# Graph attention over a dense adjacency: one fill order for the search, and the adjacency turned from a bfloat16 copy

## The chip, the cores and the metric

The kernel runs on one core of one Trainium2 chip. The metric is the device time of one execution in microseconds (us). Engines are named as in the profile: PE is TensorE's matmul and PEld its weight load, DVE is VectorE, ACT is ScalarE, POOL is GpSimd, SP is SyncE, which issues DMAs.

## The reference

Two layers over 3327 nodes with 128 features and a 0/1 adjacency. Each layer is added to its input and normalised.

```python
# layer 0
norm2 = jnp.linalg.norm(x, axis=1, keepdims=True)
cos = beta[0] * (x @ x.T) / (norm2 @ norm2.T + 1e-07)
P = softmax(cos + (1.0 - adj) * -1e9, axis=1)
x = layernorm(x + P @ x)
# layer 1: 128 attention heads of width 8
q = (x @ Wq.T).reshape(d, n, h)          # d = 128 heads, h = 8
k = (x @ Wk.T).reshape(d, n, h)
v = (x @ Wv.T).reshape(d, n, h)
a = jnp.einsum('dnh,dmh->dnm', q, k) * d ** -0.5
a = softmax(a + adj + adj, axis=2)
out = jnp.einsum('dnm,dmh->dnh', a, v).reshape(n, h * d)
x = layernorm(x + out @ Wo.T)
```

So layer 1 adds twice the adjacency to the scores, and its softmax needs the maximum of q.k over all nodes, or a bound for it.

## The kernel before

Nodes are padded to 26 tiles of 128. Node p * 26 + t is row p of tile t.

**Layer 0** runs over tiles with a software pipeline written out by hand (the loop at L418; the orders of PE, ACT, DVE and POOL are as written, SP's is not). In iteration t, tile t gets its scores, tile t - 1 its weights and their product, tile t - 2 its norm, tile t - 3 its projections to q, k, v. Tile t + 2 has its adjacency turned: `adj_chunk` (L207) transposes 26 blocks of the float32 tile `raw` on PE, four to a bank (`turn`, L159), ACT copies each bank into the bfloat16 tile `aT` (L213), and a DMA stores it to `aT_s` (L215). `raw` comes by a DMA from SP's queue (`load_adj`, L113), after POOL has set its padding column.

**Preparation** (`prepare`, L794) makes split copies of k and q by head: a DMA loads 16 heads into `nat`, POOL reorders them into `by_t`, PE transposes, ACT and DVE write a high and a low part, and DMAs store them to `kp_s` and `qp_s`. There are 16 such pieces. The first maxima of attention are put between them, and so are the loads of the first two units and of the first block's adjacency.

**Attention** runs over 288 units: a unit is one of nine blocks of query nodes (384 wide, the last 256) with four heads. A unit has 26 steps, one for each tile of key nodes (the loop at L872). The step does this, in this order on PE:

- `shifts` and `scores` of heads 2 and 3 into the two banks of `eb`; ACT exponentiates both at once into `pb` (L893), and POOL multiplies `pb` by the exponentiated adjacency `eT` (L894).
- `shifts` and `scores` of heads 0 and 1 into `ea`, then `add_adj`, which adds twice the adjacency on PE (L677); ACT exponentiates each of the two banks into `pa` (L923).
- `weigh` of the step two back: the products with the values, summed in the bank `acc` (L707).

Between these, PE also computes products q.k for the maxima of a later unit, 33 steps ahead, and DVE reduces them: `max_pair` (two heads into two banks, L613, L624) and `max_single` (one head into one bank, L634, L638). `max_steps` (L568) lists one pair and one single for each step in rounds of 52 steps, two units. Heads sit on row groups of the array, head a on rows 32a to 32a + 31. Where the pair's heads are 0 and 1, the pair stands between the shifts and scores of `eb` and the single between those of `ea`; otherwise the other way round:

```python
early = pair is not None and pair[1] == (0, 1)
```

At j = 20 of a unit `values_turn` turns the output of the unit before into a free corner of `ea`, and `finish` has ACT copy it, DVE take reciprocals (L741), POOL multiply (L742) and SP store it. `shift_parts` (L645) makes the shifts from the maxima at places 26 and 51 of the round, and at j = 22 to 24 `shift_turn` turns them.

**The end** (L949) loads the output rows, transposes them, multiplies by Wo, and adds x1 for each of the 26 tiles; then `layernorm` (L129) runs over all of them, and the result is stored. Here no engine's order is written by hand.

Of the kernel before, what the change touches and what calls it, by code (L numbers as in the profile page):

```python
# [46 lines left out]
def gnn_two_layers(  # L47
# [20 lines left out]
    nc.vector.tensor_scalar_mul(two, ident, 2.0)  # L68

# [11 lines left out]
    aT_s = dram.tile([T, P, T, P], BF16, name="aT_s")  # L81
# [31 lines left out]
    def load_adj(pool, t: int):  # L113

        raw = pool.tile([P, NP], F32, name="raw")
        nc.gpsimd.memset(raw[:, N:NP], PAD)  # L116
        if t < T - 1:
            nc.sync.dma_start(raw[:, :N], node_rows(adj, t, N))
        else:
            for a, b in FULL:  # L120
                nc.sync.dma_start(raw[a:b, :N], node_rows(adj, t, N, b - a, a))
            nc.sync.dma_start(raw[P - 1 : P, :N], node_rows(adj, t - 1, N, 1, P - 1))
        return raw
# [5 lines left out]
    def layernorm(dst: bass.AP, src: bass.AP):  # L129

        stats = small.tile([P, T, nc.vector.BN_STATS_DIM], F32, name="ln_stats", bufs=1)
        mv = small.tile([P, T, nc.vector.BN_AGGR_DIM], F32, name="ln_mv", bufs=1)
        rstd = small.tile([P, T], F32, name="ln_rstd", bufs=1)
        for t in range(T):
            nc.vector.bn_stats(stats[:, t, :], src[:, t, :])
            nc.vector.bn_aggr(mv[:, t, :], stats[:, t, :])
        nc.vector.tensor_scalar(rstd, mv[:, :, 1], EPS, None, op0=ALU.add)
        nc.scalar.activation(rstd, rstd, AF.Sqrt)
        nc.vector.reciprocal(rstd, rstd)
        for t in range(T):  # L140
            nc.vector.tensor_scalar(
                dst[:, t, :],
                src[:, t, :],
                mv[:, t, 0:1],
                rstd[:, t : t + 1],
                op0=ALU.subtract,
                op1=ALU.mult,
            )
# [24 lines left out]
    with ExitStack() as l0:  # L173
# [23 lines left out]
        def load(t: int):  # L197
            u = tiles[t]
            u.raw = load_adj(adj_raw, t)
            u.xr = ptp.tile([P, D], F32, name="xr", bufs=5)  # L200
            if t < T - 1:
                nc.sync.dma_start(u.xr, node_rows(x, t, D))
            else:
                nc.gpsimd.memset(u.xr, 0.0)
                nc.sync.dma_start(u.xr[: P - 1], node_rows(x, t, D, P - 1))

        def adj_chunk(t: int, c: int):  # L207

            u = tiles[t]
            if c == 0:  # L210
                u.aT = ptp.tile([P, T, P], BF16, name="aT", bufs=1)
            tp, a, b = turn(ps_tp, lambda k: every(u.raw, k), c)
            nc.scalar.copy(u.aT[:, a:b, :], tp)  # L213
            if c == NCH - 1:
                nc.sync.dma_start(aT_s[t], u.aT)  # L215
# [143 lines left out]
        with tc.manual_schedule(  # L359
# [25 lines left out]
            for t in range(3):  # L385
                load(t)
            ws = []
# [30 lines left out]
            for t in range(-2, T + 3):  # L418
# [4 lines left out]
                for k in range(8):  # L423
# [42 lines left out]
                    if k == 5 and there(t + 3) and t >= 0:  # L466
                        load(t + 3)

# [7 lines left out]
    with ExitStack() as at:  # L476
# [28 lines left out]
        def load_adj_tile(b, j):  # L505
            w = width(b)
            nc.sync.dma_start(
                aT[:, j, :w].rearrange("p (q n) -> p q n", n=P),
                aT_s[b * QT : b * QT + w // P, :, j].rearrange("q p n -> p q n"),
            )  # L510
# [57 lines left out]
        def max_steps(u, w):  # L568
# [18 lines left out]
            ones = one(u, hi, full[13:] + [left]) + one(u, lo, full[12:] + [left])  # L587
            pairs += [(u, hi, *k) for k in full[:13]] + [(u, hi, (2,), 6)]
            pairs += [(w, hi, *k) for k in full[:12]]
            ones += one(w, lo, full[13:] + [left])  # L590
            pairs += [(w, lo, *k) for k in full[:13]]
            ones += one(w, hi, full[12:] + [left])
            assert len(pairs) == len(ones) == 2 * T
            return list(zip(pairs, ones))
# [33 lines left out]
        def max_single(i, hs, qs, c):  # L628
# [6 lines left out]
            else:  # L635
# [7 lines left out]
                )  # L643

# [60 lines left out]
        def weigh(u, j, pts):  # L705
            for h in range(4):
                nc.tensor.matmul(  # L707
                    acc[32 * h : 32 * h + H + 1, : u.nq],
                    u.vt[:, h, j],
                    pts[h // 2][:, h % 2, : u.nq],  # L710
                    start=(j == 0),
                    stop=(j == T - 1),
                    tile_position=(0, 32 * h),
                )
# [20 lines left out]
        def finish(u, src):  # L735
            of = sm.tile([P, QT, 4, H + 1], F32, name="of")
            nc.scalar.copy(of[:, : u.nt].rearrange("p q h r -> p (q h r)"), src[:, : 36 * u.nt])
            by = of.rearrange("p q h r -> p h q r")[:, :, : u.nt]
# [23 lines left out]
        with tc.manual_schedule(  # L762
# [27 lines left out]
            with ExitStack() as pr:  # L790
# [3 lines left out]
                def prepare(g, src, dst):  # L794
                    nat = work.tile([P, HG, T * H], F32, name="nat")
                    nc.sync.dma_start(nat, heads(src)[g])
# [4 lines left out]
                    )  # L801

# [23 lines left out]
                for g in range(NG):  # L826
                    for src, dst in ((k_s, kp_s), (q_s, qp_s)):
                        prepare(g, src, dst)
                        for _ in range(3 if g > 1 else 0):
                            if k < T + AHEAD:  # L830
                                first_max(k)
                                k += 1
                    if g == 0:
                        us[0], us[1] = load_unit(0), load_unit(1)
                        for j in range(T):
                            load_adj_tile(0, j)
                    if 0 < g < 5:
                        for j in range(7 * (g - 1), min(7 * g, T)):
# [15 lines left out]
            unit = fix.tile([P, P], BF16, name="unit")  # L854
            nc.vector.tensor_copy(unit, ident)
# [16 lines left out]
            for s in range(NU * T + LAG):  # L872
                i, j = divmod(s, T)
                u = us.get(i)
                if u is not None:
# [6 lines left out]
                    early = pair is not None and pair[1] == (0, 1)  # L882
# [3 lines left out]
                    shifts(u, b01, (2, 3))  # L886
                    if early:
                        max_pair(*pair)
                    elif single is not None:
                        max_single(*single)  # L890
                    scores(u, j, b01, (2, 3), True)
# [9 lines left out]
                    shifts(u, e_a, (0, 1))  # L901
                    if early:
                        max_single(*single)
                    elif pair is not None:
                        max_pair(*pair)
                    scores(u, j, e_a, (0, 1), False)
# [9 lines left out]
                    if j == T - 6 and done is not None:  # L916
                        values_turn(done, free, False)
                        copies.append(lambda: finish(done, free))
# [7 lines left out]
                    todo.append((u, j, (pt_a, pt_b)))  # L926
# [19 lines left out]
            finish(done, e[:, 0])  # L946


    with ExitStack() as fi:  # L949
# [7 lines left out]
        hid = big.tile([P, T, D], F32, name="hid1")  # L957
        for t in range(T):
# [19 lines left out]
            nc.vector.tensor_add(hid[:, t, :], pp, x1)  # L978
        res = big.tile([P, T, D], F32, name="res")
        layernorm(res, hid)  # L980
        rf = res.rearrange("p t d -> p (t d)")
        for part, width in node_parts():
            nc.sync.dma_start(node_blocks(out, part, width), rf[part, :width])
# [38 lines left out]
```

## Time and profile before

| | us |
|---|---|
| Median of 3 runs (15734.61 to 15738.93) | 15735.61 |
| The profiled execution | 15731.62 |
| Its span, first to last instruction | 15729.8 |
| Stage: layer 0, start included | to about 712 |
| Stage: preparation | 712 to 986 |
| Stage: attention | 986 to about 15616 |
| Stage: the end | to 15729.8 |

The profile is of one execution. In a line of a group come the line of the kernel, engine, operation, what is written and read with its shape, and how often; then busy time in all and mean nanoseconds of one; then the idle time of the engine just before, and what ended it. In a timeline the first two numbers are start and length in us, and brackets hold the idle time before it. The ends of matmuls are modelled, so it is their starts that are read. "Place" below is the place in a round of 52 steps of the maxima that a step computes.

### The profile page before, as it was taken

Reading aid. Unit: us, or ns where it says so; the run is one execution under the profiler, and the core shown is the slowest. Engines: PE = TensorE matmul, PEld = TensorE weight load, DVE = VectorE, ACT = ScalarE, POOL = GpSimd, SP = SyncE. Lnnn points to the kernel's source line nnn. Section 1 sums busy time; section 2 is a strip of 40 time slices with the busy share of each in tenths; the row PEclk is TensorE's granted clock in tenths of the full one; section 3 lists DMA queues with packets and bytes.
Section 4 is the critical chain, followed back from the end, with each engine's and each line's share of the span. In section 5 each row is a group of like instructions: output and inputs, shape, how many; then the busy total and the mean of one; then the engine's idle time right before and its main releaser. Section 6 shows DMA issues by size and latency. Waiting matters only on the chain.

```text
span 15729.8 us, 508048 instructions
## 1 busy us (share of the span) xinstructions
PE 15442.3 (98%) x217532; PEld 6909.7 (44%) x217532; DVE 13882.2 (88%) x16261; ACT 12687.4 (81%) x24930; POOL 13894.1 (88%) x9571
## 2 busy tenths in 40 slices
PE   8879999999999999999999999999999999999999
PEld 6644444444444444444444444444444444444555
DVE  7679999999999999999999999999999999998775
ACT  7658888888888888888888888888888888888776
POOL 0059999999999999999999999999999999999886
PEclk9989999999999999999999999999999999999999
DMA  4451111111111111111111111111111111111112
GB/s 169 180 201 49 45 49 52 49 46 49 52 50 49 47 50 52 49 45 49 52 49 46 49 53 48 50 45 56 45 49 45 49 52 49 46 49 60 61 56 74
DMA packets 600521, 951.50 MB, mean 60 GB/s; under 512 B 283090, under 2 KB 515408, under 8 KB 557808
## 3 DMA queue, kind: packets, MB, share of 16 engines
q1 hardware_dynamic: 598256, 918.99, 18.0%
q8 instruction: 1703, 27.90, 0.7%
q14 instruction: 562, 4.60, 0.1%
HBM read 784.19 MB, written 134.61 MB: 58 GB/s over the span
## 4 chain that ended last, share of the span: by engine, by line
PE 91%; DVE 2%; ACT 1%; issue 0%; POOL 0%; DMA 0%; SPq 0%; ACTq 0%; DVEq 0%; POOLq 0%
PE acc L707 29%; PE ea L677 20%; PE m L598 15%; PE eb L690 12%; PE ea L690 9%; PE ea L696 2%; PE eb L696 2%; PE ea L663 1%; DVE mx L613 1%; PE ea L725 1%; DVE mx L634 1%; ACT pa L923 0%; PE pp L977 0%; POOL pb L894 0%; ACT pb L893 0%
## 5 line engine op out<-in xcount | busy, mean ns | idle before, releaser
L894 POOL TENSOR_TENSOR pb<-pb,eT 128x768 f32<-128x768 f32 (+1 forms) x7488 | 13206.6, 1781 | 752.7 <-ACT pb L893 557.7
L613 DVE TENSOR_REDUCE mx<-m 128x2 f32<-128x1024 f32 x6784 | 8271.6, 1219 | 506.9 <-PE eb L696 283.1
L893 ACT ACTIVATE pb<-eb 128x768 f32<-128x768 f32 (+1 forms) x7488 | 5895.6, 787 | 2509.9 <-PE eb L696 1716.6
L598 PE MATMUL m<-kx,qx 32*128 32x512 f32 (+1 forms) x23296 | 6774.5, 471 | 85.9 <-DVE mx L613 78.2
L923 ACT ACTIVATE pa<-ea 128x384 f32<-128x384 f32 (+1 forms) x14976 | 6339.0, 478 | 56.5 <-PE ea L677 43.5
L707 PE MATMUL acc<-pb,vt 128*9 128x384 f32 (+1 forms) x29952 | 5904.2, 474 | 0.1
L707 PE MATMUL acc<-pa,vt 128*9 128x384 f32 (+1 forms) x29952 | 5903.3, 474 | 0.0
L634 DVE TENSOR_REDUCE mx<-m 128x1 f32<-128x512 f32 x6400 | 4377.6, 684 | 682.2 <-PE m L598 316.3
L690 PEld LDWEIGHTS <-one 3*128 3x128 bf16 x29952 | 1508.1, 91 | 5553.9 <-issue 4650.8
L677 PE MATMUL ea<-aT,two 128*32 128x384 bf16 (+1 forms) x59904 | 3716.2, 325 | 0.0
L696 PE MATMUL eb<-qx,kx 32*128 32x384 f32 (+1 forms) x14976 | 3444.5, 452 | 0.0
L696 PE MATMUL ea<-qx,kx 32*128 32x384 f32 (+1 forms) x14976 | 3439.1, 437 | 0.0
L690 PE MATMUL ea<-cx,one 3*128 3x384 bf16 (+1 forms) x14976 | 3293.0, 322 | 2.3
L598 PEld LDWEIGHTS m<-kx,qx 32*128 32x128 f32 x23296 | 2813.9, 182 | 443.7 <-DVE mx L613 123.0
L690 PE MATMUL eb<-cx,one 3*128 3x384 bf16 (+1 forms) x14976 | 2462.7, 326 | 1.3 <-ACT pb L893 0.6
L707 PEld LDWEIGHTS acc<-pa,vt 128*9 128x9 f32 x29952 | 1416.7, 91 | 781.5 <-issue 0.3
L677 PEld LDWEIGHTS <-two 128*32 128x32 bf16 x59904 | 947.0, 95 | 1415.6 <-issue 1273.6
L696 PEld LDWEIGHTS eb<-qx,kx 32*128 32x128 f32 x14976 | 1461.7, 189 | 0.0
L696 PEld LDWEIGHTS ea<-qx,kx 32*128 32x128 f32 x14976 | 1433.1, 182 | 8.0 <-issue 3.0
L707 PEld LDWEIGHTS acc<-pb,vt 128*9 128x9 f32 x29952 | 1418.8, 91 | 0.6 <-POOL pb L894 0.6
L638 DVE TENSOR_REDUCE mx<-m 128x2 f32<-128x512 f32 x1088 | 747.9, 687 | 96.3 <-PE eb L696 38.2
L116 POOL MEMSET raw<- 128x1 f32 x26 | 2.4, 98 | 559.0 <-DVE mn L260 478.2
(126 smaller groups left out, 5253.8 us busy)
## 6 DMA issues: line engine op xcount, KB each, us to landing
kx<-kp_s SPq DMA_DIRECT2D x576, 832.0 KB
vn<-v_s SPq DMA_DIRECT2D x288, 416.0 KB
qx<-qp_s SPq DMA_DIRECT2D x1024, 48.0 KB
raw<-in_adj_dram SPq DMA_DIRECT2D x25, 1663.5 KB
aT_s<-aT SPq DMA_DIRECT2D x26, 832.0 KB
aT<-aT_s SPq DMA_DIRECT2D x208, 96.0 KB
q_s<-row SPq DMA_DIRECT2D x26, 512.0 KB
k_s<-row SPq DMA_DIRECT2D x26, 512.0 KB
```

Of the source, the lines that this page charges most:

```text
L598: nc.tensor.matmul(dst, u.qx[rows(a), q * P : (q + 1) * P], u.kx[rows(a), k0:k1], start=True, stop=True,)
L613: nc.vector.tensor_reduce(u.mx[:, h, qs[0], c], m, axis=AX.X, op=ALU.max)
L634: nc.vector.tensor_reduce(u.mx[:, a, qs[0], c : c + 1], m, axis=AX.X, op=ALU.max)
L638: nc.vector.tensor_reduce(u.mx[:, a, qs[0] : qs[1] + 1, c], m.rearrange("p (q k) -> p q k", q=2), axis=AX.X, op=ALU.max,)
L663: nc.tensor.matmul(dst[r], parts[u.i % 2][:, q, h], unit, start=start, stop=True, tile_position=(0, 32 * h), skip_group_check=True,)
L677: nc.tensor.matmul(e[r, : u.nq], two[:, r], aT[:, j, : u.nq], start=False, stop=True, tile_position=(0, 32 * c), skip_group_check=True,)
L690: nc.tensor.matmul(e[:, : u.nq], one[r], u.cx[r, : u.nq], start=True, stop=False, skip_group_check=True)
L696: nc.tensor.matmul(e[:, : u.nq], u.kx[rows(a), j * P : (j + 1) * P], u.qx[rows(a), : u.nq], start=False, stop=stop, skip_group_check=True,)
L707: nc.tensor.matmul(acc[32 * h : 32 * h + H + 1, : u.nq], u.vt[:, h, j], pts[h // 2][:, h % 2, : u.nq], start=(j == 0), stop=(j == T - 1), ...
L893: nc.scalar.activation(pt_b[:, :, : u.nq], e_b[:, :, : u.nq], AF.Exp)
L894: nc.gpsimd.tensor_tensor(pt_b[:, :, : u.nq], pt_b[:, :, : u.nq], eT[:, j, : u.nq].unsqueeze(1).to_broadcast([P, 2, u.nq]), ALU.mult,)
L923: nc.scalar.activation(pt_a[:, h, : u.nq], e[:, : u.nq], AF.Exp)
```

## The change

Seven edits go together.

1. `max_steps`: the list of singles is put in another order, so that no single's head is one of the pair's heads.
2. The step: in full blocks the pair always stands first, between the shifts and scores of `eb`, and `eb` takes the two heads that are not the pair's (`hs_b`), `ea` the pair's (`hs_a`). In the last, narrower block the single stands first.
3. `values_turn` moves from j = 20 to j = 8; `finish` is split in ACT's copy (`leave`, j = 8) and the rest (j = 9).
4. Layer 0: a second load of each adjacency tile, from POOL's queue, converts it to bfloat16 (`load_bits`, two buffers), and PE turns this copy by matmuls with the bfloat16 identity `unit` as the moving operand.
5. `aT_s` is laid out by blocks of three tiles: stores go in pieces of 256 bytes, and the loads of attention get one piece per row instead of three.
6. Preparation: `nat` is loaded two pieces ahead, and the adjacency loads of the first block are spread over four pieces.
7. The end: norm for each tile in the loop; the first 20 tiles are stored from within it.

```diff
+        def load_bits(t: int):
+            u = tiles[t]
+            u.bits = adj_raw.tile([P, NP], BF16, name="bits", bufs=2)
+            load_adj(u.bits, nc.gpsimd, t)
...
-            tp, a, b = turn(ps_tp, lambda k: every(u.raw, k), c)
-            nc.scalar.copy(u.aT[:, a:b, :], tp)
+            a, b = 4 * c, min(4 * c + 4, T)
+            tp = ps_tp.tile([P, 4, P], F32, name="tp")
+            for k in range(a, b):
+                nc.tensor.matmul(tp[:, k - a], every(u.bits, k), unit, start=True, stop=True)
+            nc.scalar.copy(u.aT[:, a:b, :], tp[:, : b - a])
             if c == NCH - 1:
-                nc.sync.dma_start(aT_s[t], u.aT)
+                q = t % QT
+                nc.sync.dma_start(aT_s[t // QT][:, :, q * P : (q + 1) * P], u.aT)
...
             for t in range(3):
                 load(t)
+            for t in range(2):
+                load_bits(t)
...
                     if k == 5 and there(t + 3) and t >= 0:
                         load(t + 3)
+                if there(t + 4) and t + 4 > 1:
+                    load_bits(t + 4)
...
-            nc.sync.dma_start(
-                aT[:, j, :w].rearrange("p (q n) -> p q n", n=P),
-                aT_s[b * QT : b * QT + w // P, :, j].rearrange("q p n -> p q n"),
-            )
+            nc.sync.dma_start(aT[:, j, :w], aT_s[b][:, j, :w])
...
-            ones = one(u, hi, full[13:] + [left]) + one(u, lo, full[12:] + [left])
+            last = one(w, hi, full[12:] + [left])
+            ones = one(u, hi, full[13:] + [left]) + last[:1] + one(u, lo, full[12:] + [left])
             pairs += [(u, hi, *k) for k in full[:13]] + [(u, hi, (2,), 6)]
             pairs += [(w, hi, *k) for k in full[:12]]
-            ones += one(w, lo, full[13:] + [left])
             pairs += [(w, lo, *k) for k in full[:13]]
-            ones += one(w, hi, full[12:] + [left])
+            ones += one(w, lo, full[13:] + [left]) + last[1:]
...
-                    early = pair is not None and pair[1] == (0, 1)
+                    full = pair is not None and width(units[pair[0]][0]) == QB
+                    first = pair if full else single
+                    late = single if full else pair
+                    hs_a = pair[1] if full else (0, 1)
+                    hs_b = tuple(h for h in range(4) if h not in hs_a)
...
-                    shifts(u, b01, (2, 3))
-                    if early:
-                        max_pair(*pair)
-                    elif single is not None:
-                        max_single(*single)
-                    scores(u, j, b01, (2, 3), True)
+                    shifts(u, b01, hs_b)
+                    search(first)
+                    scores(u, j, b01, hs_b, True)
...
-                    shifts(u, e_a, (0, 1))
-                    if early:
-                        max_single(*single)
-                    elif pair is not None:
-                        max_pair(*pair)
-                    scores(u, j, e_a, (0, 1), False)
+                    shifts(u, e_a, hs_a)
+                    search(late)
+                    scores(u, j, e_a, hs_a, False)
...
-                    if j == T - 6 and done is not None:
+                    if j == 8 and done is not None:
                         values_turn(done, free, False)
-                        copies.append(lambda: finish(done, free))
+                        copies.append(lambda: leave(done, free))
+                    if j == 9 and done is not None:
+                        copies.append(lambda: finish(done))
...
+                load_heads(0)
+                load_heads(1)
+                for i in range(len(works)):
+                    prepare(i)          # load_heads(i + 2) after POOL's copy
+                    if i == 1:
                         us[0], us[1] = load_unit(0), load_unit(1)
...
+                    if i % 2 and i < 9:
+                        for j in range(7 * (i // 2), min(7 * (i // 2) + 7, T)):
                             load_adj_tile(0, j)
...
-            nc.vector.tensor_add(hid[:, t, :], pp, x1)
-        res = big.tile([P, T, D], F32, name="res")
-        layernorm(res, hid)
+            hid = work.tile([P, D], F32, name="hid1")
+            nc.vector.tensor_add(hid, pp, x1)
+            layernorm(res[:, t, :], hid)
+            if t == HALF - 1:
+                nc.sync.dma_start(node_blocks(out, slice(0, P), HALF * D), rf[:, : HALF * D])
```

`layernorm` now takes one tile: bn_stats, bn_aggr, the addition of epsilon, ACT's root, reciprocal, and the final scaling.

## The prediction

> **What bounds the kernel now.** I read the page first, then busy time by stage, then the timeline of single attention steps, then groups with shapes kept apart.
>
> ```profile
> PE 15442.3 (98%) x217532; PEld 6909.7 (44%) x217532; DVE 13882.2 (88%) x16261; ACT 12687.4 (81%) x24930; POOL 13894.1 (88%) x9571
> ...
> PE 91%; DVE 2%; ACT 1%; issue 0%; POOL 0%; DMA 0%; SPq 0%; ACTq 0%; DVEq 0%; POOLq 0%
> ```
>
> TensorE carries the chain, but four engines stand above 80%, so the reader must ask stage by stage what holds it.
>
> ```profile
> 65.00:712.00 647.00, 611.95 (x3399) 478.46 (x3397) 541.27 (x830) 508.54 (x655) 2.40 (x24) 0.99 0.42 160
> 712.00:986.00 274.00, 121.33 (x540) 90.64 (x540) 135.93 (x215) 74.28 (x142) 51.37 (x30) 0.62 0.98 338
> ...
> 1083.00:14330.00 13247.00, 13225.12 (x189035) 5551.74 (x189031) 12085.33 (x13709) 10957.05 (x21294) 12610.58 (x8389) 1.00 0.16 49
> ...
> 15612.00:15704.00 92.00, 74.40 (x632) 66.29 (x620) 29.51 (x93) 16.05 (x31) 2.92 (x4) 0.94 0.58 173
> 15704.00:15729.80 25.80, 7.91 (x65) 7.24 (x64) 11.01 (x41) 3.26 (x5) 0.00 (x0) 0.76 0.21 69
> ```
>
> Columns: window, length, busy PE, PEld, DVE, ACT, POOL, clock, DMA share, GB/s. Layer 0 (to 712) is TensorE; the preparation of keys and queries (to 986) is the DMA engines, 0.98 busy; attention is 84% of the span; the end has a 26 us tail in which little runs.
>
> In attention a step is the distance between starts of eb<-cx,one on PE: 7488 steps. The full-width 6656 average 2.005 us, in rounds of 52 (two units). By place in the round they differ. In 26 places the pair search comes before the eb scores and the single before the ea scores ("pair first"), in the other 26 the reverse. Both settle at the same pace, in pairs of steps. For single first I read a loop over two steps: eb start to single reduction 0.538, to pair reduction 0.608, that one 1.215, to the next pair product 0.055, to the eb after it 1.517: 3.933, or 1.967 a step. For pair first: 0.554 + 1.137 + 0.683 + 0.057 + 1.511 = 3.942, or 1.971. So the banks that the search keeps until VectorE has reduced them set the pace, not TensorE's arithmetic alone. What stands out is where the order turns round:
>
> ```profile
> 5066.98 1.22 DVE L613 TENSOR_REDUCE mx<-m 128x2 f32<-128x1024 f32 x1
> ...
> 5067.75 0.34 PE L690 MATMUL eb<-cx,one 3*128 3x384 bf16 x2
> 5068.25 0.50 PE L598 MATMUL m<-kx,qx 32*128 32x512 f32 x2 [0.16 <-DVE mx L613]
> 5068.25 0.44 PE L696 MATMUL eb<-qx,kx 32*128 32x384 f32 x2
> ...
> 5068.79 1.23 DVE L613 TENSOR_REDUCE mx<-m 128x2 f32<-128x1024 f32 x1 [0.60 <-PE m L598]
> ...
> 5070.12 0.34 PE L690 MATMUL eb<-cx,one 3*128 3x384 bf16 x2
> ```
>
> A pair late in one step and first in the next: PE stands 0.50 us after its shifts until VectorE frees the two banks, VectorE then stands 0.60 us, and the step takes 2.37 us.
>
> **The change, part by part.**
>
> *Constant order, and singles of other heads.* Mean steps at places 12 to 15 are 2.161, 2.198, 2.060, 1.880, together 0.42 over four of 1.969; here the order turns and pair and single share a head (place 12: ea scores 0.33 us apart instead of together). Places 39 to 41, the other turn with the second clash just before it: 2.353, 2.067, 1.875, 0.39 over. The new code always puts the pair first, between the shifts and scores of the other two heads, and no single has a head of its pair. Both waits have no cause left: -0.81 a round. Against it, 26 steps move from 1.967 to 1.971: +0.10. There are 8 x 32 / 2 = 128 rounds: 128 x 0.71 = **-91 us**.
>
> *Output turn moved from j = 20 to 8, its finish split.* In pair-first steps places 0 to 6 (the maxima's parts, the output turn, three shift turns) cost 0.59 over the steady step, in single-first steps the same work at 27 to 32 costs 0.37. All steps become pair first: +0.22. The split takes away a wait: VectorE's reciprocal stood 0.42 us for ScalarE's copy (5098.59); one step later the copy is done. The 24 small matmuls keep their 0.21 us on PE, and the copy still holds the ea bank. I take 0.1 saved a unit, 0.2 a round: **0** net; both ends -0.3 and +0.2 a round, -38 to +26 us. Queued behind the reciprocal is the next pair reduction, which it no longer holds up. POOL, 1.80 us a product back to back against steps of 1.97, absorbs its share in either place.
>
> *Adjacency turned from a bfloat16 copy.*
>
> ```profile
> L690 PEld LDWEIGHTS <-one 3*128 3x128 bf16 x29952 | 1508.1, 91 | 5553.9 <-issue 4650.8
> ...
> L164 PE MATMUL tp<-ident,raw 128*128 128x128 f32 x676 | 100.4, 290 | 12.7 <-ACT aT L213 12.7
> ...
> L164 PEld LDWEIGHTS tp<-ident,raw 128*128 128x128 f32 x676 | 90.7, 199 | 25.5 <-ACT aT L213 14.9 <-issue 5.5 <-PE acc L298 5.0
> ...
> L213 ACT CAST aT<-tp 128x512 bf16<-128x512 f32 x156 | 86.3, 587 | 47.3 <-PE tp L164 47.3
> ```
>
> A tile takes 24.26 us, PE without a break; its 26 transposes start 0.115 apart. The new matmul streams 128 bfloat16 columns once. Not in this trace: from below, four of L677's 384 columns start each 0.163, so 128 would take 0.054; from above 0.115, no gain (a loss would need a load longer than the float32 one's 199 ns, which it isn't). The nearest weight load, 128 bfloat16 columns, lasts 91 ns, but loads overlap. [...] 26 x 0.6 = **-15 us**, -30 to 0.
>
> *The load of that copy, on POOL's queue.* Each tile is read a second time, 1663 KB. Its pad memset waits for PE's reads two tiles back; behind it on POOL stands only the next raw tile's memset, for which SP's load waits. Issued at a tile's end, it is needed 41 us later (24.26 and the 17 until the turning begins). The raw load of the same bytes takes 4.6 us of all 16 engines (packet times of 300 to 400 us), and the DMA share is 0.42: hidden. [...] VectorE is busy 541 of 647 us here. [...] No run here shows such a load. At the start it isn't hidden: the first 35 us are DMA-bound (packet share near 1 from 10 us), POOL waits 20.17 us for the squares' input, and two more tiles join: 3.3 MB at the 400 GB/s seen there is 8 us; **+7 us**, 0 to +12. The store of the turned tile goes in 256-byte pieces: 3328 at the 18 ns that 256-byte packets take here, over 16 engines, 3.7 us against 2.1; aT is written again some 17 us later, so 0, though the attention loads then become one piece of 768 bytes.
>
> *Preparation: loads two ahead.* SP's order is not written by hand and already ran ahead: a nat load issued at 841.4 was used at 864. Only the second one stood behind the units' and adjacency loads (POOL waits 41.1 us for nat<-k_s), but the DMA engines were full meanwhile. To win is what the packets left empty, mostly at 720, 770, 940 and 980 us: about 15 us, and some 3 from larger adjacency pieces. **-10 us**, -18 to 0.
>
> *End: norm per tile, output in two parts.* From the last add (15713.23) to the end are 16.2 us. The tile's own chain is 1.9 us (0.29, 0.29, 0.17, 0.18, 0.23, 0.32, 0.34 and gaps), then three issues of 0.4 and a smaller landing, perhaps 3: 6. **-9 us**. In the tiles before, VectorE idles 2.06 us before each add, which hides the extra 1.2 us, if the next copy from PSUM goes ahead of them; in this trace it goes between bn_stats and bn_aggr. If not, the end below.
>
> Sum: -91 - 15 + 7 - 10 - 9 = **-118 us**. The profiled execution took 15731.6 us (span 15729.8 and 1.8 around it), 4.0 under the median 15735.6. So 15613.6, as a median 15617.6.
>
> **Rivals.** (1) The turns' waits only give back slack: a late pair costs a step what its neighbours then win, and other engines refill it. For: places 15 and 41 run short (1.88) after the long ones. Against: the 0.81 is net of those. Attention then gives 0: 15735.6 - 27 = 15709. (2) The converted load is starved: above 41 us from issue to landing each tile waits. The load and the 7 us of turning fill two tiles: at 60 us a tile takes 33.5, +9.2 x 26 = +240 over the rest's -103: 15873, slower. It turns slower than before from (103 / 26 + 24.26) x 2 - 7 = 49 us. [...] (3) The norm stands in front of the copy that feeds TensorE: 1.5 us on 25 tiles, +38 instead of -9: 15665.
>
> **How the numbers follow.** Forecast 0.68, its own range 15545 to 15690; rival (1) 0.14, (2) 0.05, (3) 0.13. Predicted 15617. The bounds of the terms, not all at one end, give 15535 to 15695; outside lie most of (1) and (2). The measurement tells about 0.2%, 31 us: (1) lies half beyond it. Faster 0.68 + 0.13 + 0.07 = 0.88, same 0.07, slower 0.05.
>
> **What would show it.** Right: full-width steps average 1.99; no step of 2.2 at the turns; DVE's idle before L634 falls; tiles at 23.7 us; the first inverse_log a few us later; no long POOL wait for nat; no row of TENSOR_SCALARs at the end. Wrong: steps still near 2.005, or PE waiting for the converted tile.

## The result, and the profile after

The changed kernel takes 15611.48 us (median of 4 executions, 15607.61 to 15613.94), the kernel before beside it on the same chip 15735.11 (15732.48 to 15738.93): a ratio of 0.9921, 95% interval 0.9909 to 0.9933. In five later executions (a_again), beside nine of the kernel before, it was 15607.64 and 0.992 (0.9906 to 0.9933). So the change saves 0.8%, clear of the noise; the forecast was 15617 us, and faster.

The profiled execution took 15613.45 us, span 15611.6: 118.2 us less span, where the prediction's sum said 118. So good a hit is partly luck, as the stages show. First the page after: busy time, the chain's shares, and the DMA issues of the two adjacency loads (KB each, us to landing).

```profile
PE 15342.4 (98%) x217532; PEld 6892.6 (44%) x217532; DVE 13898.5 (89%) x16311; ACT 12601.3 (81%) x24955; POOL 13899.2 (89%) x9625
...
PE 93%; DVE 0%; issue 0%; ACT 0%; DMA 0%; POOL 0%; SPq 0%; POOLq 0%; ACTq 0%; DVEq 0%
...
raw<-in_adj_dram SPq DMA_DIRECT2D x25, 1663.5 KB, 6.5
...
bits<-in_adj_dram POOLq DMA_DIRECT2D x25, 831.8 KB, 7.2
```

PE executes as many matmuls as before and is busy for 99.9 us less, at the same share (the ends of matmuls are modelled, so part of their waits counts as busy). DVE's share of the chain went from 2% to 0%. The converted load, the one thing that was feared to make the change slower, lands after 7.2 us in the median (13.4 at the most). Then busy time by stage after (window, length, busy PE, PEld, DVE, ACT, POOL, clock, DMA share, GB/s):

```profile
65.00:700.00 635.00, 591.64 (x3414) 456.34 (x3413) 544.53 (x832) 511.72 (x660) 17.88 (x72) 0.98 0.68 194
700.00:984.00 284.00, 136.87 (x547) 95.27 (x545) 135.76 (x213) 76.29 (x145) 51.38 (x30) 0.60 0.95 325
1083.00:14230.00 13147.00, 13146.09 (x189195) 5559.52 (x189187) 12100.45 (x13717) 10878.25 (x21319) 12607.26 (x8396) 1.00 0.16 50
```

In attention PE now has 0.9 us idle in 13147, against 22 us in 13247 before. The stages, from the two traces (us; inverse_log is ScalarE's logarithm, once for each tile of layer 0; the first line is the start of the last one, "tail" runs from there to the issue of the last v_s store, "preparation" from there to the first attention step):

| | before | after | difference | predicted |
|---|---|---|---|---|
| Last inverse_log | 639.73 | 631.16 | -8.6 | -8 |
| Layer 0's tail | 79.0 | 84.5 | +5.5 | 0 |
| Preparation | 267.8 | 268.6 | +0.8 | -10 |
| Attention, first to last step | 14626.0 | 14520.8 | -105.2 | -91 |
| From there to the end | 117.4 | 106.7 | -10.7 | -9 |

Attention won 14 us more than predicted, the stages before it 16 less. The full-width steps average 1.9892 us (2.0054 before). The step at place 39 of the round, which took 2.37 us in the prediction's timeline, now takes 1.96. Timeline after, of PE:

```profile
4001.19 0.34 PE L700 MATMUL eb<-cx,one 3*128 3x384 bf16 x2
...
4001.20 0.50 PE L604 MATMUL m<-kx,qx 32*128 32x512 f32 x2
...
4001.23 0.47 PE L706 MATMUL eb<-qx,kx 32*128 32x384 f32 x2
...
4001.64 0.44 PE L706 MATMUL ea<-qx,kx 32*128 32x384 f32 x2
...
4003.15 0.34 PE L700 MATMUL eb<-cx,one 3*128 3x384 bf16 x2
```

The pair's products start 0.01 us after the shifts and the eb scores 0.03 us after those: nobody waits for the pair's banks any more. At places 13 and 39 the first search starts on average 0.004 us behind the first shift, where before it was 0.33 and 0.48. The groups of DVE's two reductions (busy, mean ns | idle before, what ended it), before and then after, show where its waiting went.

```profile
L613 DVE TENSOR_REDUCE mx<-m 128x2 f32<-128x1024 f32 x6784 | 8271.6, 1219 | 506.9 <-PE eb L696 283.1 <-PE m L598 121.5
...
L634 DVE TENSOR_REDUCE mx<-m 128x1 f32<-128x512 f32 x6400 | 4377.6, 684 | 682.2 <-PE m L598 316.3 <-PE eb L696 271.0
```

```profile
L619 DVE TENSOR_REDUCE mx<-m 128x2 f32<-128x1024 f32 x6784 | 8312.5, 1225 | 970.0 <-PE eb L706 568.7 <-PE m L604 64.3
...
L640 DVE TENSOR_REDUCE mx<-m 128x1 f32<-128x512 f32 x6400 | 4360.3, 681 | 258.5 <-PE m L604 239.9 <-PE eb L706 17.8
```

Before these two together it did not fall: 1189 us became 1229. Most of it stands before the pair now, which comes first in every step. Over the attention windows (13247 and 13147 us) DVE's idle time fell from 1162 to 1047 us, since the same work fills a shorter stretch. A good part of that is the wait of its reciprocals in full blocks (79 us before, most of it for ScalarE's copy; none after), and e1 below shows that this part won no time.

### The profile page after: what moved, and what is told of

It is laid out like the page before. It is cut to its first block, busy times and chain, and to the rows that moved or that the text cites. A ratio compares the mean times of both kernels' runs of the same rounds, so it can differ in the third digit from the quotient of the medians.

```text
span 15611.6 us, 508271 instructions
## 1 busy us (share of the span) xinstructions
PE 15342.4 (98%) x217532; PEld 6892.6 (44%) x217532; DVE 13898.5 (89%) x16311; ACT 12601.3 (81%) x24955; POOL 13899.2 (89%) x9625
## 3 DMA queue, kind: packets, MB, share of 16 engines
q1 hardware_dynamic: 625024, 918.99, 18.3%
## 4 chain that ended last, share of the span: by engine, by line
PE 93%; DVE 0%; issue 0%; ACT 0%; DMA 0%; POOL 0%; SPq 0%; POOLq 0%; ACTq 0%; DVEq 0%
PE acc L717 30%; PE ea L687 21%; PE m L604 16%; PE eb L700 13%; PE ea L700 10%; PE ea L706 2%; PE ea L673 1%; PE ea L735 1%; PE eb L706 1%; PE pp L1006 0%; DVE oT L147 0%; DMA qp_s<-low 0%; ACT pa L946 0%; PE tp L157 0%; DVE hid L1008 0%
## 5 line engine op out<-in xcount | busy, mean ns | idle before, releaser
L604 PE MATMUL m<-kx,qx 32*128 32x512 f32 (+1 forms) x23296 | 6873.5, 472 | 80.5 <-DVE mx L619 71.5
L946 ACT ACTIVATE pa<-ea 128x384 f32<-128x384 f32 (+1 forms) x14976 | 6338.4, 478 | 54.0 <-PE ea L687 14.5
L700 PEld LDWEIGHTS <-one 3*128 3x128 bf16 x29952 | 1469.1, 91 | 5634.9 <-issue 4656.0
L706 PE MATMUL ea<-qx,kx 32*128 32x384 f32 (+1 forms) x14976 | 3326.9, 434 | 0.0
L700 PE MATMUL ea<-cx,one 3*128 3x384 bf16 (+1 forms) x14976 | 2744.1, 324 | 1.0
L706 PEld LDWEIGHTS ea<-qx,kx 32*128 32x128 f32 x14976 | 1396.3, 182 | 7.3 <-issue 3.7
L630 DVE TENSOR_REDUCE mx<-m 128x4 f32<-128x1024 f32 x288 | 352.8, 1225 | 46.7 <-PE m L604 28.6
```

The lines of the kernel that those rows point to most:

```text
L604: nc.tensor.matmul(dst, u.qx[rows(a), q * P : (q + 1) * P], u.kx[rows(a), k0:k1], start=True, stop=True,)
L630: nc.vector.tensor_reduce(dst, m.rearrange("p a (x k) -> p a x k", x=2), axis=AX.X, op=ALU.max)
L700: nc.tensor.matmul(e[:, : u.nq], one[r], u.cx[r, : u.nq], start=True, stop=False, skip_group_check=True)
L706: nc.tensor.matmul(e[:, : u.nq], u.kx[rows(a), j * P : (j + 1) * P], u.qx[rows(a), : u.nq], start=False, stop=stop, skip_group_check=True,)
L946: nc.scalar.activation(pt_a[:, h, : u.nq], e[:, : u.nq], AF.Exp)
```

## Experiments

Each kernel is the changed one with the edits shown. Most were executed once, and layer 0's tail alone moves a total by up to 10 us (below), so stages are compared and not totals. Attention, in the nine profiled kernels whose attention code is the changed kernel's, took 14510.4 to 14520.8 us (mean 14515.7), so differences of some 5 us there say nothing. Their preparation, where its code too was the changed one, took 264.2 to 269.9.

### The output turn put back: e1_turn_back

```diff
-                    if j == 8 and done is not None:
+                    if j == T - 6 and done is not None:
                         values_turn(done, free, False)
                         copies.append(lambda: leave(done, free))
-                    if j == 9 and done is not None:
                         copies.append(lambda: finish(done))
```

> The changed kernel with one part put back: the output turn stands at j = 20 again and its copy and reciprocal follow each other in one step. Attention (first to last start of eb<-cx,one) took 14626.0 us before and 14520.8 after. Theory (order and singles carry the attention's gain, the place of the output turn carries nothing): 14510 to 14535, round of 52 steps 103.4 to 103.6. Rival (a good part of the gain is the output turn's new place, away from the maxima's parts and the shift turns, and its split): 14545 to 14570, round 103.6 to 103.85. The steps with the output turn move from places 15 and 41 of the round to 27 and 1, and cost there 0.2 to 0.4 us over their neighbours.

Attention took 14516.0 us, the round 103.42: with order and singles in place, the output turn is worth nothing at either j. It costs 2.26 us at place 27 and 2.29 at place 1 (2.24 and 2.18 at 15 and 41 in the changed kernel). The rival is out. Against before, order and singles together carry 14626.0 - 14516.0 = 110 us.

### The two halves of that: e2_singles_only and e3_order_only

e2 has the old order and the new list of singles; e3 the new order and the old list. Both have the output turn at j = 20.

```diff
# e2
-                    first = pair if full else single
-                    late = single if full else pair
-                    hs_a = pair[1] if full else (0, 1)
+                    early = pair is not None and pair[1] == (0, 1)
+                    first = pair if early else single
+                    late = single if early else pair
+                    hs_a = (0, 1)
```

> The changed kernel with its attention as before, but for the list of singles: no single search has a head of its step's pair, while the order of pair and single still turns round twice a round (14626.0 us of attention before, 14520.8 after; 2.0054 and 1.9892 us a full-width step). Theory (shared heads and turning order each cost, and add up): 14565 to 14605; places 12 and 38 lose their excess, 13 and 39 keep a step above 2.15. Rival A (only the turning order costs): 14615 to 14630. Rival B (only the shared head costs, the turn falls where it does by chance): 14520 to 14545, and no step above 2.15 at places 13 and 39. Rival C (each alone gives slack back, both are needed): over 14610 here and in the run with the order alone.

```diff
# e3
-            last = one(w, hi, full[12:] + [left])
-            ones = one(u, hi, full[13:] + [left]) + last[:1] + one(u, lo, full[12:] + [left])
+            ones = one(u, hi, full[13:] + [left]) + one(u, lo, full[12:] + [left])
...
-            ones += one(w, lo, full[13:] + [left]) + last[1:]
+            ones += one(w, lo, full[13:] + [left])
...
+            ones += one(w, hi, full[12:] + [left])
```

> The changed kernel with its attention's pair always first and its singles in the old list: at places 12 and 38 of the round the single shares a head with the pair, and stands between the shifts and scores of that same head; the output turn is at j = 20. Theory (both add up): 14540 to 14580 us of attention, together with the run of the singles alone some 105 us below twice 14626; places 12 and 38 0.1 to 0.3 us above their neighbours, none at 13 and 39. Rival A (only the turning order costs): 14515 to 14535. Rival B (only the shared head costs): 14615 to 14630. Rival C (both are needed): over 14610.

| attention, us | old order | constant order |
|---|---|---|
| old singles | 14626.0 (before) | 14550.7 (e3) |
| new singles | 14623.4 (e2) | 14516.0 (e1) |

They don't add up: the order is worth 75 us alone, the list 3 us alone, which is within the spread, and 35 beside the order. My additive theory gave the order alone 46 to 86 and the list alone 21 to 61, so it held for e3 and failed for e2. By e2 alone only the turning order would cost (rival A), but e3 lies outside rival A's range. Places 12 to 15 of the round say why:

| place | 12 | 13 | 14 | 15 | sum |
|---|---|---|---|---|---|
| before | 2.161 | 2.198 | 2.060 | 1.879 | 8.298 |
| e2, new singles | 1.984 | 2.375 | 2.064 | 1.878 | 8.301 |
| e3, new order | 2.149 | 1.877 | 2.058 | 1.886 | 7.970 |
| e1, both | 1.976 | 2.030 | 1.907 | 2.029 | 7.942 |

In e2 the shared head at place 12 is gone and the step is 0.18 us shorter, but the next is 0.18 longer. Its timeline (place 13 starts at 4172.18; x is how many lie together):

```profile
4171.95 0.68 DVE L640 TENSOR_REDUCE mx<-m 128x1 f32<-128x512 f32 x1
...
4172.18 0.34 PE L700 MATMUL eb<-cx,one 3*128 3x384 bf16 x2
...
4172.68 0.49 PE L604 MATMUL m<-kx,qx 32*128 32x512 f32 x1 [0.17 <-DVE mx L640]
...
4173.21 0.69 DVE L640 TENSOR_REDUCE mx<-m 128x1 f32<-128x512 f32 x1 [0.58 <-PE m L604]
...
4174.54 0.34 PE L700 MATMUL eb<-cx,one 3*128 3x384 bf16 x2
```

A single stands late in step 12 and first in step 13, and there is one bank for it: its product waits until DVE has reduced the last one, at 4172.63. PE comes to that bank earlier, thanks to the free step before, and only waits the longer: at place 13 the single starts on average 0.51 us behind the first shift, 0.33 before. So the shared head had been paid inside the wait at the turn. Without that wait it shows, as in e3 at place 12:

```profile
4154.31 0.49 PE L603 MATMUL m<-kx,qx 32*128 32x512 f32 x1
4154.31 0.65 PE L705 MATMUL ea<-qx,kx 32*128 32x384 f32 x2
```

In the changed kernel two ea scores take 0.44 us together (4001.64 above); here 0.65, because one of them stands behind the single on the same rows of the array: it starts 0.33 us after the other on average, where in the changed kernel they start together.

### The output turn alone: e4_turn_only

Both edits of e2 and e3 undone, `values_turn` at j = 8 and the rest of `finish` at j = 9.

> The changed kernel with the order of pair and single and the list of singles as before, and the output turn at j = 8 with its finish a step later. Theory (its place carries nothing, the prediction's term of 0): attention 14615 to 14640 us (14626.0 before), the output turn's 0.2 to 0.3 us only moving from places 1 and 27 to 15 and 41. Rival (the place carries part of the gain): 14570 to 14600. Other rival (at place 41 it meets the turning order and the waits add up): over 14650.

Attention took 14611.5 us: 14.5 less than before, between the two cases I had written down, and a miss for both. The long steps move from places 1 and 27 (2.289 and 2.151) to 41 and 15 (2.093 and 2.096), where before had steps of 1.875 and 1.879 behind the turns. Where the output turn left (places 0 to 6 and 27 to 32) the round gets 0.51 us shorter, where it came (12 to 15 and 39 to 41) 0.42 longer; in the changed kernel against e1 the same two sums are 0.52 and 0.44. The two moves differ in the steps behind place 15: places 16 to 26 get 0.07 us shorter here and 0.05 longer there. So the move is worth 14.5 us beside the old order and nothing beside the new one; why is not shown.

### The adjacency turned from float32 again: e5_raw

```diff
-            for t in range(2):
-                load_bits(t)
...
-                nc.tensor.matmul(tp[:, k - a], every(u.bits, k), unit, start=True, stop=True)
+                nc.tensor.transpose(tp[:, k - a], every(u.raw, k), ident)
...
-                if there(t + 4) and t + 4 > 1:
-                    load_bits(t + 4)
```

> The changed kernel with the adjacency turned by float32 transposes from the raw tile again and without the second load; the turned tile is still stored in 256-byte pieces. Theory (the matmul from the bfloat16 copy is what shortens the tile, the two early converted loads are what delays the start): tile period 24.2 to 24.3 us (24.263 before, 23.567 after), first inverse_log back at 49 to 51 us (49.31 and 56.06), last one 638 to 641 (639.73 and 631.16). Rival (another thing of this part shortens the tile, such as the store's layout or the adjacency loads in one piece): period 23.5 to 23.7.

Period 24.269 us, first inverse_log at 49.12, last at 639.63: each is back at the value of before, so this part of the change makes all of the -0.70 us a tile and all of the +6.75 at the start; the store in 256-byte pieces costs and gives nothing. The groups of the turned blocks, in e5 and then after:

```profile
L215 PE MATMUL tp<-ident,raw 128*128 128x128 f32 x676 | 100.3, 290 | 12.6 <-ACT aT L216 12.6
...
L216 ACT CAST aT<-tp 128x512 bf16<-128x512 f32 x156 | 86.4, 587 | 47.2 <-PE tp L215 47.2
```

```profile
L216 ACT CAST aT<-tp 128x512 bf16<-128x512 f32 x156 | 86.1, 587 | 30.7 <-PE tp L215 27.7 <-DMA aT_s<-aT 2.5
...
L215 PE MATMUL tp<-unit,bits 128*128 128x128 bf16 x676 | 67.2, 230 | 18.3 <-ACT aT L216 16.4
```

PE's busy time for them falls by a third, its idle time just before them grows from 12.6 to 18.3 us over all tiles, 16.4 of it for ScalarE's copies, and ScalarE waits less for PE: the two banks now bind more than before.

### The old preparation: e6_prep

The loop of before: each `nat` loaded directly ahead of its use, the 26 adjacency loads at once.

> The changed kernel with the preparation's loop of before (a load directly ahead of its use, all 26 adjacency loads at once). Preparation is counted from the issue of the last v_s store to the first attention step: 267.8 us before, 268.6 after, 266.6 to 268.9 in four more kernels with the changed loop. Theory (DMA engines set its length, the order of loads only moves the idle time): 266 to 270. Rival (the prediction's -10: the loads ahead do win time, and something else in the change took it back): 274 to 282.

Preparation took 270.1 us, just above the theory's range and 0.3 above the longest of the changed loop. The loads two ahead are worth nothing that these traces can tell. The long POOL wait for nat (41.1 us before) is gone after, as predicted, and back here (41.4 us), and the time did not follow. That the DMA engines set the pace fits their share (0.98 busy before, 0.95 after).

### The old end: e7_end

The norm over all tiles after the last, one output store.

> The changed kernel with the end of before (the norm over all tiles after the last, one output store). Theory (all of the end's gain lies behind the last add): from the last attention step to the end 116.5 to 118 us (117.36 before, 106.67 after), from the last add 16 to 17 (16.6 and 5.7), so the 26 tiles themselves take the same 100.7 to 101. Rival (the norm per tile slows the tiles and gives back part): the tiles get 1 us or more shorter here, below 99.8.

From the last step to the end 117.07 us, from the last add 16.69. The 26 tiles in between took 100.4 us here and 100.9 after, but 100.4 to 101.3 in the twelve kernels with the norm in the loop: it costs them nothing that can be told from the spread. The gain lies all behind the last add (5.74 us after).

### The first converted loads later: e8_start

```diff
-            for t in range(2):
-                load_bits(t)
...
             nc.gpsimd.tensor_mul(xs, xs, xs)
+            for t in range(2):
+                load_bits(t)
```

> The changed kernel with the first two converted loads issued behind POOL's product of the squares, so after about 22 us, and not at the start. Theory (at the start these 3.3 MB only displace the loads that everything waits for; the copy isn't needed before PE turns it at about 45 us): first inverse_log 49 to 52 us (56.06 after, 49.31 before), period 23.56 as after, last one 624 to 628 (631.16). Rival (the bytes must pass in any case before the first turning, so PE waits for the converted tile instead): first one 54 to 58. Other rival (POOL's descriptors for these loads stand in front of its squares of xT and delay them): over 58.

First inverse_log at 49.26 us, last at 624.05: the +6.75 us were no price of the second load, only of its place. Busy time from 30 to 40 us, after and then in e8:

```profile
30.00:40.00 10.00, 0.48 (x3) 0.49 (x4) 4.49 (x6) 0.70 (x2) 5.08 (x1) 1.00 1.00 405
```

```profile
30.00:40.00 10.00, 7.04 (x25) 5.01 (x26) 5.43 (x9) 2.47 (x5) 6.44 (x7) 1.00 1.03 299
```

The DMA engines are full in both. After, PE has nothing to do meanwhile; in e8 the same bytes pass beside its first 7 us of work.

### Layer 0's tail: e9_tail and e10_fill

The tail took 84.5 us after and 79.0 before, with the same work in it. In the tail PE projects one tile after the other through one bank, `pq`, and stands for each of ScalarE's copies. The projection's matmuls of 1061 to 1222 ns, in the last tile after, and of 592 to 697 ns in e4, at about the same time (ns minimum/median/maximum, first and last start):

```profile
L356 PE MATMUL pq<-wq,x1T x4: 1061/1141/1222, 698.8 to 702.6; 128*128 128x512 f32 x4
L357 ACT ACTIVATE row<-pq x2: 597/597/597, 700.9 to 703.7; 128x512 f32<-128x512 f32 x2
```

```profile
L356 PE MATMUL pq<-wq,x1T x4: 592/644/697, 694.6 to 697.0; 128*128 128x512 f32 x4
L357 ACT ACTIVATE row<-pq x3: 597/598/598, 691.5 to 695.8; 128x512 f32<-128x512 f32 x3
```

ScalarE takes the same 597 ns in both; PE's clock is another (after, it falls at 687.2 us, and 0.50 is granted for the rest of the tail). Each kernel runs the same projections, and they fall into three groups:

| kernel | matmuls over 1 us in the tail | tail, us |
|---|---|---|
| e4, e7 | 0 | 74.9, 74.9 |
| before, e2, e3, e5, e6 | 9 or 10 | 79.0, 79.5, 79.4, 79.4, 79.4 |
| after once more (a_again) | 11 | 80.4 |
| after, e1, e8 | 19 or 20 | 84.5, 84.2, 84.5 |

Matmuls of over 1 us begin about 56 or 66 us after the last inverse_log (64.6 once), or not at all. The changed layer 0 appears with 0, with about 10 and with 20 of them: not the change but the moment at which the clock falls decides.

```diff
# e9: three banks in the tail
-            pq = ps_x.tile([P, 512], F32, name="pq")
+            if t >= T - 2 and k % 2:
+                pq = ps_tp.tile([P, 4, P], F32, name="tp").rearrange("p a b -> p (a b)")
+            else:
+                pq = ps_x.tile([P, 512], F32, name="pq")
```

> The changed kernel, in which the projections of layer 0's last two tiles take turns on three PSUM banks (pq and the two tp banks, which are free by then) and not on pq alone. From the last inverse_log to the issue of the last v_s store it is 74.9, 79.4 or 84.4 us in the kernels so far, with 0, 9 or 10, and 19 or 20 slow projection matmuls (over 1 us). Theory (PE stands 0.7 us for each of ScalarE's copies, and its clock falls because of these stands): no slow projection, 63 to 69 us. Rival A (the clock falls for another reason, at 56 or 66 us after that inverse_log, whatever PE does): slow ones remain, 66 to 76. Rival B (another chain, the norm or ScalarE's copies, sets the tail): over 74.

```diff
# e10: PE kept busy
             nc.tensor.matmul(pq, u.x1T, ws[n][:, cols], start=True, stop=True)
+            if t >= T - 2:
+                idle = ps_tp.tile([P, 4, P], F32, name="tp").rearrange("p a b -> p (a b)")
+                nc.tensor.matmul(idle, u.x1T, ws[n][:, cols], start=True, stop=True)
```

> The changed kernel, in which each projection of layer 0's last two tiles is computed a second time into a free tp bank that nothing reads; pq is still the only bank that counts. It takes away PE's stands, not ScalarE's copies. Theory (the clock falls because PE stands): no slow projection, and the tail as in the kernels with none, 74 to 76.5 us. Rival A (the clock falls for another reason): 8 to 20 slow ones, over 79, and by up to 10 us more since each is doubled. Rival B (PE has no room for the second matmul beside the copies): over 78 with none slow.

e9: tail 65.3 us, no matmul over 1 us, preparation 269.1; the execution took 15588.5 us. e10: 74.7 us, no matmul over 1 us. Busy time from 696 to 716 us after, and in the first half of that in e10 (its tail ends at 705):

```profile
696.00:716.00 20.00, 14.21 (x15) 3.18 (x13) 0.00 (x0) 4.44 (x8) 0.94 (x6) 0.50 0.21 81
```

```profile
696.00:706.00 10.00, 9.47 (x21) 3.39 (x20) 0.00 (x0) 3.17 (x6) 0.41 (x3) 1.00 0.26 105
```

With twice the projections on PE, the tail is as short as in the kernels that had no long matmuls. That the three banks shorten the tail is shown: 65.3 is below even the undisturbed 74.9. What brings the clock down is less clear, since it falls at this stage in every one of the fourteen traces. In e4 and e7 it fell too, only 75.2 and 76.3 us after the last inverse_log, as the tail ended. Windows of e4, whose tail ends at 705.7:

```profile
686.00:696.00 10.00, 5.96 (x11) 1.62 (x11) 0.98 (x5) 3.77 (x9) 0.00 (x0) 1.00 0.42 164
696.00:716.00 20.00, 5.63 (x10) 1.49 (x10) 0.00 (x0) 3.36 (x6) 0.94 (x6) 0.75 0.62 201
```

With PE's stands left in, the clock fell within the tail in nine kernels and within 1.4 us of its end in the other two. In e9, e10 and e11 it fell 4 to 5 us behind the tail, when PE had stopped. That PE's stands bring the clock down agrees with this. It is likely and not settled: e4 ran on with the stands for some 20 us at full clock, and what picks 56, 66 or 76 us stays open.

### Three repairs together: e11_best, beside the changed kernel once more

The edits of e8 and e9, and `shift_parts` of the first unit moved behind the preparation's loop:

```diff
-                if k == T:
-                    shift_parts(us[0])
...
+                shift_parts(us[0])
                 values(us[0])
                 values(us[1])
```

> Three repairs on the changed kernel: the first two converted loads behind POOL's squares (it won 6.8 us at the start), layer 0's last projections on three banks, and the first unit's shift_parts behind the preparation's loop, where it no longer stands between two copies on POOL. Theory: first inverse_log at 49.3 us, tail 63 to 69 us, preparation 258 to 265 (264.2 to 270.1 so far; POOL's 21.7 us gap at 920 us gone), attention 14510 to 14521; together 15575 to 15592 us, 0.12 to 0.23% below the changed kernel on the same chip. Rival (the preparation is bound by the DMA engines, moving shift_parts only moves its idle time): preparation 265 to 270, total 15582 to 15600.

> The changed kernel once more, to be compared with the one with three repairs on the same chip: 15597 to 15614 us by the theory that its spread between executions comes from where the clock falls in layer 0's tail (0, 10 or 20 slow projections, 74.9, 79.4 or 84.4 us), and 0.991 to 0.993 of the kernel before.

The repaired kernel takes 15573.96 us (15570.59 to 15575.20, four executions), the changed one on the same chip 15607.64 (15603.70 to 15609.66, five): 33.7 us or 0.22% less, and a microsecond below the range that I gave; against before 0.9898 (0.9885 to 0.9912). In its trace the first inverse_log starts at 48.31, the tail is 65.3, the attention 14514.5 and the preparation 260.2, 4 us below the shortest of the others. POOL's work in the preparation after, and in the repaired kernel, says where that came from (brackets: idle before, what ended it):

```profile
916.39 2.96 POOL L819 COPY by_t<-nat 128x3328 f32<-128x3328 f32 x1 [12.63 <-PE tp L157]
940.97 0.23 POOL L665 CAST parts<-neg 128x12 bf16<-128x12 f32 x1 [21.62 <-DVE neg L658]
...
942.04 2.96 POOL L819 COPY by_t<-nat 128x3328 f32<-128x3328 f32 x1
```

```profile
915.23 2.96 POOL L820 COPY by_t<-nat 128x3328 f32<-128x3328 f32 x1 [11.43 <-DMA qp_s<-high]
928.85 2.96 POOL L820 COPY by_t<-nat 128x3328 f32<-128x3328 f32 x1 [10.67 <-PE tp L157]
945.57 0.23 POOL L668 CAST parts<-neg 128x12 bf16<-128x12 f32 x1 [13.77 <-DVE neg L661]
```

After, a 0.23 us cast stands ahead of the next copy in POOL's order and waits 21.6 us for DVE; in the repaired kernel the copies follow each other 12 to 15 us apart from 859 us on. The other two edits do not explain it: with one of them alone the preparation took 266.8 (e8) and 269.1 us (e9).

## Why the prediction was right, point by point

- **Order and singles (-91).** Right in mechanism, too small: 110 us. The waits were sized well: in e1 places 12 to 15 lost 0.36 us a round (predicted 0.42), 39 to 41 lost 0.40 (predicted 0.39; from 6.295 to 5.892). The term that failed is the +0.10 for steps that change from single first to pair first. It rested on two paces, 1.967 and 1.971, read off single loops of two steps. Places 16 to 26, which made that change, went from 1.973 to 1.963 on average: -0.11 in all. A difference of 0.004 us was below what that reading could tell. The two waits were also booked as if each stood for itself; that only worked because both were removed together (e2).
- **Output turn (0).** Right beside the new order: 14516.0 without the move, 14515.7 on average with it. The split did take DVE's wait for the copy away, but no time came of it. Beside the old order the same move was worth 14.5 us (e4), which the prediction's reasons don't give.
- **Adjacency turned (-15).** Right: -15.3 us from the first inverse_log to the last. But it is made up otherwise: 0.70 us a tile, in most of the 25 distances between two inverse_logs; the first three won nothing. The 0.6 us a tile in the forecast's sum was the author's estimate, and no run shows it. In its place the trace after shows matmuls that start 0.066 us apart in the median (0.115 before), with weight loads of 156 ns, not 91. By the medians 26 x 0.049 = 1.27 us a tile were to be had, so the waits took back 45%: in the steady tiles PE stands 0.44 us a tile for the copies of aT, 0.21 before.
- **The converted load (0 in the steady part, +7 at the start).** Right: 7.2 us to landing where 41 were to be had, +6.75 at the start. POOL's issue took 541 ns each, with VectorE busy for 544.5 of 635 us.
- **Preparation (-10).** Wrong: nothing (e6). The step that failed took the slices in which packets left the engines empty for something that earlier loads could fill. The gap near 940 us was POOL's order around `shift_parts`, which the change leaves as it was; moving that won 4 to 10 us against the other preparations (e11).
- **End (-9).** 10.7; e7 puts all of it behind the last add. The prediction's own figures, 16.2 less 6, give 10.
- **Rivals.** Attention's slack: out for the change as a whole, 105 us were kept, though for the list of singles alone it was true (e2). The starved load: out, it landed after 7.2 us in the median. The norm in front of the copy: out, the 26 tiles take no longer than the spread (e7).

The sum was right to 1 us for the profiled execution (6 us for the median) because attention's extra 14 us and the 16 us missing before it cancelled; a third of the latter is the tail's clock, which no term held.

## What to carry to other kernels

Two waits in neighbouring steps are one account: removing the smaller one alone gave 3 us here, and 35 once the larger was gone, so test them in all four combinations before dropping an edit as useless. An engine that runs in written order stops for the least important instruction in front of it, so look for what waits long and matters little (0.23 us of POOL held up 21.6 us). Place a new transfer by when its data is needed, not by where the other loads stand: the same two loads cost 6.8 us at the start and nothing behind it.

## What the hardware showed unexpectedly

The granted TensorE clock halved here behind stands of PE of no more than 1.03 us. After, PE's stands in the tail's projections began at 684.2 us, none over 1.03 us (most are 0.69), and PE was still busy for 1.29 of the 3.0 us from there to 687.2. There the clock fell to 0.50, and the matmuls went from 0.59 to 0.70 up to 1.06 to 1.22 us for the rest of the tail. A longer stand, 1.49 us up to 653.8, had left the clock at 1.00. The moment differs between kernels with the same code in this stage and moves the time by 0, 5 or 10 us, 0.06% of the whole. Anyone who compares versions of this kernel by a few microseconds has to read that stage first.
